# Moving the last weight load into the opening line of loads of a bilinear-interaction kernel, with in-place turning of the third weight part

## The chip, the cores and the metric

One core of one Trainium2 chip. The metric is the device time of one execution in microseconds (us), median over runs. The kernel is already tuned; the question is what one more rearrangement of its opening does.

## The reference, cut to what matters

```python
def _L0_rec_ref(inputs, W):          # inputs (4096, 32, 64), W (496, 64, 64), f32
    F = inputs.shape[1]
    idx_i, idx_j = np.triu_indices(F, k=1)      # 496 pairs i < j
    vi = inputs[:, idx_i, :]
    vj = inputs[:, idx_j, :]
    vidots = jnp.einsum('bpd,pde->bpe', vi, W)
    return vidots * vj                          # (4096, 496, 64) f32
```

The result is 520 MB. It is written once and dwarfs the 34 MB of x and the 8 MB of w.

## The kernel before

The batch is cut into 32 tiles of 128 rows. Per tile, 46 steps each multiply the turned x by up to 16 pairs' weights into PSUM (where TensorE's products land here, `ps<-wT,xT` in the profile), and then multiply by x again into an output buffer `ot`, of which there are three. A group of steps ends with one DMA of about 3 MB to the result. The first three tiles (`LEAD = 3`) run interleaved group by group, because w is still being prepared at that time: it comes in four parts of 128, 128, 128 and 112 pairs, one pair per partition. Each part is ordered (a strided copy into a small buffer `rp`) and turned (TensorE transposes, then a copy out of PSUM into `wT`), in four slices `k` each.

```python
    def load_w(c: int, eng=nc.sync):
        a, b = wrows[c]
        pool, tag = ((opool, "ot"), (opool, "ot"), (const, "w3"), (const, "w3"))[c]
        raw[c] = pool.tile([P, D * D], F32, tag=tag, name=f"raw_{c}")
        eng.dma_start(out=raw[c][: b - a, :], in_=wflat[a:b])
    ...
    load_x(0, nc.sync, 0, 1); load_w(0); load_w(1); load_x(0, nc.sync, 1, NB)   # joined here on one line
    load_w(2)
    new_x(1)
    load_x(1, nc.sync)
    ...
                if (c, k) == (2, NU - 1):
                    load_w(3, nc.scalar)        # the buffer w3 comes free only now
    ...
        if i in aside and c0 == 0 and s not in no_aside:    # shared product
            tmp = tpool.tile([P, CH, 2, E2], F32, tag="tmp", name=f"tmp_{s}")
            nc.scalar.copy(tmp, src)
            nc.gpsimd.tensor_mul(dst, tmp, xj)
        else:
            nc.vector.tensor_mul(dst, src, xj)
```

The third and fourth parts shared one buffer, so the fourth could be loaded only after the third had been ordered. "Shared" products are those that ScalarE and GpSimd make together in place of VectorE.

## Time and profile before

| | before |
|---|---|
| time, median of the first 3 runs | 1342.57 us |
| span in the profile | 1341.7 us |
| busy share: TensorE, VectorE, ScalarE, GpSimd | 85%, 71%, 35%, 40% |
| bytes moved | 562.86 MB, mean 420 GB/s |

How to read it: no compute engine is full (85% at most), DMA is (share 1.00 over the 1229 us from 106 on). In the lines of the profile PE is TensorE (PEld its loads of weights), DVE is VectorE, ACT is ScalarE, POOL is GpSimd, and SPq and ACTq are the queues on which SyncE and ScalarE ask for DMAs. Mean shares hide the opening, where for some microseconds it is not DMA that limits.

### The profile page before, as it was taken

The numbers are of one execution on the slowest core, as the hardware profiler recorded it, in microseconds if no ns is written. First come the engines' busy times: TensorE is split into PE (matmuls) and PEld (weight loads), VectorE is DVE, ScalarE is ACT, GpSimd is POOL, SyncE is SP. The second block draws the span as 40 slices with busy tenths as digits, with TensorE's granted clock in tenths as the row PEclk, the third lists the DMA queues.
The fourth block names the chain that finished last, engine by engine and source line by source line (L and its number), as shares of the span: only waits on it lengthen the run. The fifth ranks groups of instructions, "written<-read, shape, count | busy, mean of one in ns | idle before, by whom it ended". The sixth has DMA issues, their size and how long they took to land.

```text
span 1341.7 us, 16676 instructions
## 1 busy us (share of the span) xinstructions
PE 1137.5 (85%) x6656; PEld 605.0 (45%) x6656; DVE 954.2 (71%) x1262; ACT 467.7 (35%) x623; POOL 543.0 (40%) x252
## 2 busy tenths in 40 slices
PE   5989888878798797998888988788897879988884
PEld 3545444444344444444444544344444435444442
DVE  4778777767677676776767777577775767777774
ACT  4443333333233342333333333333333323333331
POOL 1723343444334443343453434434334433444441
PEclk9989999989999898998999999899998999999997
DMA  9899999999999999999999999999999999999997
GB/s 383 347 428 419 418 425 427 431 422 430 422 432 431 420 430 421 431 424 432 424 415 430 421 432 426 417 430 408 425 429 429 427 421 428 418 416 431 429 432 320
DMA packets 28895, 562.86 MB, mean 420 GB/s; under 512 B 3537, under 2 KB 3537, under 8 KB 3825
## 3 DMA queue, kind: packets, MB, share of 16 engines
q1 hardware_dynamic: 24176, 530.59, 93.0%
q10 hardware_dynamic: 2576, 20.71, 3.8%
q0 software_dynamic: 2064, 10.50, 2.0%
q8 instruction: 52, 0.85, 0.2%
q14 instruction: 27, 0.21, 0.0%
HBM read 41.68 MB, written 520.09 MB: 419 GB/s over the span
## 4 chain that ended last, share of the span: by engine, by line
DMA 55%; PE 22%; DVE 14%; POOL 5%; issue 2%; ACT 1%; SPq 0%; DVEq 0%; POOLq 0%; ACTq 0%
DMA out_dram<-ot 53%; PE ps L248 20%; DVE ot L265 13%; POOL ot L263 4%; DMA xs<-in_r_inputs_dram 2%; PE ptx L146 2%; ACT tmp L262 1%; PE ptw L134 1%; DVE rp L124 0%; POOL rp L124 0%; ACT xT L150 0%; ACT xT L152 0%; ACT xT L151 0%; DVEq L265 0%; POOL xs L100 0%
## 5 line engine op out<-in xcount | busy, mean ns | idle before, releaser
L265 DVE TENSOR_TENSOR ot<-ps,xs 128x1024 f32<-128x1024 f32 (+15 forms) x1252 | 940.9, 807 | 357.1 <-DMA out_dram<-ot 214.9
L248 PE MATMUL ps<-wT,xT 64*128 64x512 f32 (+13 forms) x6016 | 1046.1, 488 | 167.9 <-DVE ot L265 163.3
L263 POOL TENSOR_TENSOR ot<-tmp,xs 128x1024 f32<-128x1024 f32 x220 | 519.4, 2362 | 770.7 <-ACT tmp L262 592.6
L248 PEld LDWEIGHTS ps<-wT,xT 64*128 64x128 f32 x6016 | 534.7, 195 | 620.3 <-DVE ot L265 372.8
L262 ACT COPY tmp<-ps 128x1024 f32<-128x1024 f32 x220 | 222.7, 1012 | 498.0 <-PE ps L248 462.5
L150 ACT COPY xT<-ptx 128x512 f32<-128x512 f32 x128 | 74.9, 585 | 322.8 <-PE ptx L146 322.8
L146 PE MATMUL ptx<-ident,xs 128*128 128x128 f32 x512 | 84.8, 289 | 13.8 <-DMA xs<-in_r_inputs_dram 8.8
L146 PEld LDWEIGHTS ptx<-ident,xs 128*128 128x128 f32 x512 | 54.2, 142 | 85.9 <-DVE ot L265 60.0
L152 ACT COPY xT<-ptx 64x512 f32<-64x512 f32 x128 | 74.5, 582 | 1.5
L151 ACT COPY xT<-ptx 64x512 f32<-64x512 f32 x128 | 73.9, 577 | 1.5
L134 PE MATMUL ptw<-ident,rp 128*128 128x128 f32 (+1 forms) x128 | 19.1, 304 | 4.8 <-DVE rp L124 4.8
L134 PEld LDWEIGHTS ptw<-ident,rp 128*128 128x128 f32 (+1 forms) x128 | 16.1, 160 | 12.5 <-issue 5.4
L138 ACT COPY wT<-ptw 128x1024 f32<-128x1024 f32 (+1 forms) x15 | 14.8, 984 | 20.0 <-PE ptw L134 16.1
L124 DVE COPY rp<-raw 128x1024 f32<-128x1024 f32 (+1 forms) x9 | 12.8, 1453 | 10.6 <-DMA raw<-in_L_rec_W_dram 10.6
L100 POOL DMA_DIRECT2D xs<-in_r_inputs_dram x15 | 9.5, 636 | 0.0
L124 POOL COPY rp<-raw 128x1024 f32<-128x1024 f32 x4 | 8.0, 1990 | 0.1
L124 ACT COPY rp<-raw 112x1024 f32<-112x1024 f32 (+1 forms) x3 | 5.8, 1949 | 4.6 <-POOL ot L263 2.7
L92 POOL DMA_DIRECT2D scratch<-in_r_inputs_dram x7 | 6.2, 888 | 0.3 <-issue 0.3
L138 DVE COPY wT<-ptw 128x1024 f32<-128x1024 f32 x1 | 1.2, 1224 | 2.5 <-PE ptw L134 2.5
L150 ACT ACT_TABLE_LOAD x1 | 1.3, 1283 | 0.7 <-PEq L289 0.7
masks.py:199 POOL TENSOR_SCALAR_AFFINE_SELECT ident<-ident 128x128 f32<-128x128 f32 x1 | 0.3, 292 | 0.1
masks.py:197 POOL MEMSET ident<- 128x128 f32 x1 | 0.2, 204 | 0.3 <-POOLq L289 0.3
(4 smaller groups left out, 0.4 us busy)
## 6 DMA issues: line engine op xcount, KB each, us to landing
out_dram<-ot SPq DMA_DIRECT2D x64, 3360.0 KB, 16.4
out_dram<-ot SPq DMA_DIRECT2D x32, 3168.0 KB, 15.9
out_dram<-ot SPq DMA_DIRECT2D x32, 3104.0 KB, 17.0
out_dram<-ot SPq DMA_DIRECT2D x31, 2880.0 KB, 16.9
xs<-in_r_inputs_dram ACTq DMA_DIRECT2D x9, 2048.0 KB, 25.4
xs<-in_r_inputs_dram POOLq DMA_DIRECT2D x5, 1920.0 KB, 25.0
raw<-in_L_rec_W_dram SPq DMA_DIRECT2D x3, 2048.0 KB, 13.8
xs<-in_r_inputs_dram SPq DMA_DIRECT2D x2, 1024.0 KB, 10.3
```

The costliest lines, as they stand in the source:

```text
L100: tc.keep_in_program_order(nc.gpsimd.dma_start(out=dst[ps, :, fs, :], in_=rows[ps, :, fs, :]))
L124: copy(rp[:r], src[:, k * EU : (k + 1) * EU])
L134: nc.tensor.transpose(pt[:, n, :r], rp[:r, n].rearrange("p h d -> p (h d)"), ident[:r, :r])
L138: copy(wT[home][:, o : o + r, k * EU : (k + 1) * EU], pt[:, :, :r].rearrange("p e r -> p r e"))
L146: nc.tensor.transpose(pt[:, u, :], xs[blk][:, k, f : f + 2, :].rearrange("p f d -> p (f d)"), ident)
L150: copy(xT[:, 0], pt)
L151: copy(xT[D:, 1], pt[:D])
L152: copy(xT[:D, 1], pt[D:])
L248: nc.tensor.matmul(ps[:, h, lo - pa : hi - pa, :], xT[blk, kt, i // RUN][h * D : (h + 1) * D, (i + h) % 2, i % RUN // 2, :], wT[home][h * ...
L262: nc.scalar.copy(tmp, src)
L263: nc.gpsimd.tensor_mul(dst, tmp, xj)
L265: nc.vector.tensor_mul(dst, src, xj)
```

## The change

The intent is to load the fourth part of w at the start, where DMA has a hole. For this the third part's raw rows are loaded straight into the place where its turned form will lie (so buffer w3 is free for the fourth part from the beginning), block 1 of x goes ahead of the third part, the ordering and turning are spread over other steps, and the shared products of the first three tiles use the output buffer itself as their middle stop, since the small buffers are all taken by `rp`.

```diff
     def load_w(c: int):
         a, b = wrows[c]
-        pool, tag = ((opool, "ot"), (opool, "ot"), (const, "w3"), (const, "w3"))[c]
+        if c == 2:
+            raw[c] = home_of(c).rearrange("p r e -> p (r e)")
+        else:
+            pool, tag = (const, "w3") if c == 3 else (opool, "ot")
...
-        copy(rp[:r], src[:, k * EU : (k + 1) * EU])
+        ins = copy(rp[:r], src[:, k * EU : (k + 1) * EU])
+        if c > 0:
+            tc.keep_in_program_order(ins)
...
-        (2, (17, 22, 27, 32), (19, 24, 29, 34)),
-        (3, (54, 54, 55, 55), (57, 60, 63, 66)),
+        (2, (16, 18, 25, 27), (30, 33, 36, 39)),
+        (3, (46, 48, 50, 52), (56, 59, 62, 65)),
...
-    load_w(2)
     new_x(1)
     load_x(1, nc.sync)
+    load_w(2)
+    load_w(3)
...
-                if (c, k) == (2, NU - 1):
-                    load_w(3, nc.scalar)
...
-        if i in aside and c0 == 0 and s not in no_aside:
-            tmp = tpool.tile([P, CH, 2, E2], F32, tag="tmp", name=f"tmp_{s}")
+        if i in aside and c0 == 0:
+            tmp = dst
+            if t >= LEAD:
+                tmp = tpool.tile([P, CH, 2, E2], F32, tag="tmp", name=f"tmp_{s}")
```

(`home_of` returns the part's place in the turned weights; `no_aside`: the list of steps without shared products.)

More of the change, by code (lines that the diff above doesn't have):

```diff
@@ L111, with home_of, load_w @@
     NU = E2 // EU
-    def load_w(c: int, eng=nc.sync):
-        a, b = wrows[c]
-        pool, tag = ((opool, "ot"), (opool, "ot"), (const, "w3"), (const, "w3"))[c]
-        raw[c] = pool.tile([P, D * D], F32, tag=tag, name=f"raw_{c}")
-        eng.dma_start(out=raw[c][: b - a, :], in_=wflat[a:b])
+    def home_of(c: int):
+        home, tag, n = (wrows[3][0], "w3", NP - wrows[3][0]) if c == 3 else (0, "w", wrows[3][0])
+        if home not in wT:
+            wT[home] = const.tile([P, n, E2], F32, tag=tag, name=f"wT_{home}")
+        return wT[home][:, wrows[c][0] - home : wrows[c][1] - home, :]
+    def load_w(c: int):
+        a, b = wrows[c]
+        if c == 2:
+            raw[c] = home_of(c).rearrange("p r e -> p (r e)")
+        else:
+            pool, tag = (const, "w3") if c == 3 else (opool, "ot")
+            raw[c] = pool.tile([P, D * D], F32, tag=tag, name=f"raw_{c}")
+        nc.sync.dma_start(out=raw[c][: b - a, :], in_=wflat[a:b])
     def order_w(c: int, k: int, copy):
@@ L128, in turn_w @@
         r = wrows[c][1] - wrows[c][0]
-        home, tag, n = (wrows[c][0], "w3", r) if c == 3 else (0, "w", wrows[3][0])
-        if home not in wT:
-            wT[home] = const.tile([P, n, E2], F32, tag=tag, name=f"wT_{home}")
         pt = psum.tile([P, EU, P], F32, tag="ps", name=f"ptw_{c}_{k}")
@@ L136, in turn_w @@
             )
-        o = wrows[c][0] - home
-        copy(wT[home][:, o : o + r, k * EU : (k + 1) * EU], pt[:, :, :r].rearrange("p e r -> p r e"))
+        copy(home_of(c)[:, :, k * EU : (k + 1) * EU], pt[:, :, :r].rearrange("p e r -> p r e"))
     def turn_x(blk: int, k: int, q: int, copy):
@@ L192 @@
             due.setdefault(turns[k], []).append(("turn", c, k))
-    no_aside = range(52, 67)
     LATE = 6
@@ L233 @@
                 c, k = args
-                rps[c, k] = order_w(c, k, (v, v, p, v)[c] if k % 2 == 0 else (v, v, p, a)[c])
-                if (c, k) == (2, NU - 1):
-                    load_w(3, nc.scalar)
+                rps[c, k] = order_w(c, k, ((v, v, p, v), (v, v, p, a))[k % 2][c])
         base, end = groups[g]
```

## The prediction

> **What bounds the kernel now.** I read the page's slices first, then the kernel cut into stretches with the DMA share of each, then the order of events around the holes. From the page, the slices of the span (33.5 us each):
>
> ```profile
> PE   5989888878798797998888988788897879988884
> ...
> DMA  9899999999999999999999999999999999999997
> GB/s 383 347 428 419 418 425 427 431 422 430 422 432 431 420 430 421 431 424 432 424 415 430 421 432 426 417 430 408 425 429 429 427 421 428 418 416 431 429 432 320
> ...
> HBM read 41.68 MB, written 520.09 MB: 419 GB/s over the span
> ```
>
> No engine is full, but DMA is, in all slices except the first two and the last. 93% of the bytes are the result, which nothing in the diff makes smaller. So the time is bytes by rate plus the time in which DMA is idle or slow, and the diff touches only the first 100 us. A longer list of stretches shows where the loss is (columns: stretch, length, busy time of PE, PEld, DVE, ACT, POOL with instruction counts, granted clock, DMA share, GB/s):
>
> ```profile
> 28.00:36.00 8.00, 8.00 (x36) 4.14 (x35) 5.15 (x6) 3.77 (x5) 0.74 (x1) 0.79 0.89 368
> 36.00:39.00 3.00, 3.00 (x20) 1.74 (x18) 2.93 (x4) 1.01 (x1) 2.94 (x2) 1.00 0.02 7
> 39.00:60.00 21.00, 21.00 (x121) 11.43 (x118) 15.34 (x16) 10.13 (x10) 17.43 (x9) 1.00 0.99 418
> 60.00:66.00 6.00, 6.00 (x35) 2.97 (x35) 4.14 (x5) 3.77 (x5) 3.65 (x3) 1.00 1.04 316
> 66.00:104.00 38.00, 32.66 (x202) 19.04 (x200) 29.21 (x36) 16.99 (x20) 11.19 (x5) 0.91 1.00 428
> 104.00:106.00 2.00, 2.00 (x16) 0.99 (x14) 2.00 (x4) 1.34 (x3) 1.27 (x1) 1.00 0.62 260
> 106.00:1335.00 1229.00, 1051.53 (x6172) 555.39 (x6168) 882.04 (x1187) 418.84 (x568) 501.73 (x228) 0.95 1.00 425
> 1335.00:1341.70 6.70, 0.00 (x0) 0.00 (x0) 0.00 (x0) 0.00 (x0) 0.00 (x0) 0.50 0.05 21
> ```
>
> The reader is to see three places below 425 GB/s besides the two ends: a hole at 36 to 39 us where nothing is in flight, a slow stretch at 60 to 66 that is nevertheless full, and a small hole at 104 to 106. From 106 on DMA is full at 425. Cut into 2 us pieces, the first hole shows its edges too (26 to 28 us moved 193 GB/s, 34 to 36 moved 204, 38 to 40 moved 184).
>
> What happens there, from the timeline of engines and of the SP queue, and from the chain of waits:
>
> ```profile
> 3.33 24.41 DMA xs<-in_r_inputs_dram
> 27.73 0.14 issue
> 27.87 0.63 PE ptx L146 x4
> ```
> ```profile
> 38.50 0.33 SPq L270 DMA_DIRECT2D out_dram<-ot  x1
> 45.36 0.33 SPq L270 DMA_DIRECT2D out_dram<-ot  x1
> 52.64 0.33 SPq L270 DMA_DIRECT2D out_dram<-ot  x1
> 60.80 0.33 SPq L270 DMA_DIRECT2D out_dram<-ot  x1
> ```
> ```profile
> 58.47 0.40 ACTq L118 DMA_DIRECT2D raw<-in_L_rec_W_dram  x1
> ```
>
> The loads asked for at the start end near 27 us. Two small writes follow (issued at 27.2 and 29.2), and then DMA waits for the compute engines until tile 1's first group is finished at 38.5. TensorE itself waits for block 1 of x until 27.87, since that is last in the line of loads. And w's fourth part, 1792 KB, is loaded only at 58.5, into traffic that is full already.
>
> [...] the load on ACT's queue at 58.5 shares the time with writes and landed about 14.8 us later. [...] VectorE's two copies of w's second part at 21.95 took 4.16 us together while GpSimd multiplied (2.66 us), the one at 34.33 with GpSimd free took 1.05.
>
> **The change part by part.**
>
> 1. The fourth part of w joins the line of loads, and block 1 of x moves ahead of the third part. Nothing is added in bytes; 1792 KB (1.835 MB) move from the busy stretch at 58.5 to the hole. At 425 GB/s they take 4.3 us. The line now ends near 27.0 + 4.3 = 31.3 us, and the first two writes (1952 and 928 KB, 4.7 + 2.2 us), already waiting, follow without the 1 us gap at 27, to 38.2. The next write must be issued about 0.6 us before that, by 37.6. In the kernel before it comes at 38.5.
>
> 2. Block 1 of x lands 4.9 us earlier (it no longer stands behind 2048 KB: 2.097 MB by 425 GB/s), near 22.8 instead of 27.7. TensorE was idle 2.97 us before 27.87 for it. VectorE, the fuller engine at this time, was idle 1.43 and 1.42 us before its multiplies at 30.61 and 33.25, both of which come after that wait; so I take 2.8 us off the 38.5: about 35.7, in time for 37.6. The next (2880 KB, 6.9 us of transfer) is due by 44.5 and should come near 41.5 instead of 45.36. So the hole closes: VectorE and TensorE lead DMA by 2 to 3 us.
>
> 3. What the hole is worth: from 24 to 40 us the eight 2 us pieces moved 438, 193, 500, 375, 393, 204, 11 and 184, mean 287 GB/s, against 425: 16 x 138 / 425 = 5.2 us.
>
> 4. The stretch at 60 to 66: 6 x (425 - 316) / 425 = 1.5 us. It is there only while the fourth part is read among writes, whereas reads in the opening line ran at 411 over 3 to 28 us, edges included. I count 1.5 us as gained, with less certainty.
>
> 5. The hole at 104 to 106: 2 x (425 - 260) / 425 = 0.8 us. It follows the stretch in which ordering (VectorE 2.60 and 1.03 us, ScalarE 1.93 and 1.96) and turning w's fourth part (four times about 1.0 to 1.5 us of TensorE) stood in the steps of tiles 1 and 2, after a wait for the late load. The ordering now comes four to eight steps earlier and its data has long been there. I count it as gained.
>
> 6. Third part turned in place: the same 4 copies on GpSimd (1.99 us), 32 transposes and 4 copies out of PSUM (1.01 us); added is one wait, that all four ordering copies are read before the first turn writes over the raw rows. Those fall at steps 16, 18, 25 and 27, the turn at step 30. GpSimd has 4 x 2.0 + 4 x 2.36 = 17.4 us of work from step 14 to step 27, whereas in the timeline before TensorE takes about 14 us over these steps. By my walk through them the turn waits until 54 us or so, some 2 us late, and tile 1's second group ends near 57.5 for a deadline of about 59. So it is near the path, not on it.
>
> 7. Shared products of the first tiles in the output buffer: 4 multiplies (steps 53, 58, 62, 66) move from VectorE (about 1.1 us each) to ScalarE (1.01) plus GpSimd (2.36). It frees the four small buffers. A ScalarE copy that begins a group must now wait for the output buffer to come free; there the kernel waits for that anyway. Nothing counted.
>
> Sum: 5.2 + 1.5 + 0.8 = 7.5 us at best. A check from the bytes: 562.86 MB at 425 is 1324.4 us, plus 2.5 lost in the first 4 us (45 and 283 GB/s in its halves), plus 6.4 after 1335, gives 1333.3 of span; with the 7.5 it is 1340.8, against a span of 1341.7. So nothing large is missing. I give back 1.4 us for new small gaps (points 6 and 7): 1342.57 - 7.5 + 1.4 = 1336.5 us.
>
> **The rivals.** (a) The gain is only an earlier backlog, and the compute engines, which lose their slack, bring it back later. For it: PE is 85% busy, and later stretches have small dips too (330 GB/s in 1150 to 1154). Against: 1229 us at a share of 1.00. It would leave 1340 to 1342. (b) GpSimd becomes the bound in the opening: the in-place wait holds TensorE by more than my 2 us, in front of three writes of 7.5 us, and the hole reappears around 55 to 65. For it: 17.4 us of work in 14. Against: a lead of 2 to 3 us, and the bytes put ahead. It would give back 2 to 4 us: 1338 to 1341. (c) Only the hole is worth something, the slow stretch is noise of mixed traffic: 1337 to 1338. (d) A different phase of reads against writes moves the rate of 425 by 0.3%, which is 4 us in either direction; nothing in the profile decides that.
>
> **Range and chances.** Rivals a to c pull up, d both ways; best case 1333. So 1333 to 1340.5 eight times in ten. 2% would be 27 us; the whole loss outside the full stretch is under 17 us, so faster by 2% is out of reach, and slower would need a lasting block: 0.01 and 0.01.
>
> **What would show it.** Right: DMA share near 1.00 from 3 to 106 us, no stretch at 7 GB/s; the third output write issued before 37.6 us; no stretch near 316 GB/s after 58 us; 106 us onward still at 425; the write of tile 0's third group issued some 7 us earlier relative to the bytes moved. Wrong: a hole in the list of 2 us pieces after 50 us with TensorE waiting for GpSimd's ordering copies (b), new dips after 106 (a), or a steady rate off 425 by more than 1 GB/s (d).

## The result, and the profile after

The changed kernel took 1338.51 us (median of 4 runs, 1338.19 to 1339.52), the kernel before 1343.04 in the same rounds: ratio 0.9968, 95% interval 0.9953 to 0.9983. Ratios here are the mean time of one kernel's fast runs over the mean of the other's fast runs of the same rounds, so they are not quite the ratio of the medians. The gain is clear of noise and small: 4.5 us by the medians.

The slices of the page of the changed kernel (33.4 us each):

```profile
GB/s 371 431 429 425 426 420 429 423 428 431 424 429 420 421 430 423 431 420 427 432 407 430 424 431 425 422 426 405 429 426 428 426 418 427 422 415 430 430 429 318
```

The second slice went from 347 to 431 GB/s. The first, however, fell from 383 to 371. The stretches that the prediction listed, now for the changed kernel (stretch, length, busy time of PE, PEld, DVE, ACT, POOL, granted clock, DMA share, GB/s):

```profile
28.00:36.00 8.00, 7.02 (x40) 3.54 (x37) 7.63 (x7) 3.53 (x4) 2.36 (x1) 1.00 0.98 325
36.00:39.00 3.00, 2.73 (x15) 1.34 (x16) 3.00 (x4) 0.62 (x1) 0.00 (x0) 1.00 0.95 405
39.00:60.00 21.00, 21.00 (x120) 11.40 (x120) 16.12 (x17) 9.87 (x12) 20.53 (x10) 1.00 1.02 438
60.00:66.00 6.00, 6.00 (x40) 3.60 (x38) 3.80 (x5) 4.23 (x5) 3.93 (x3) 1.00 1.00 430
66.00:104.00 38.00, 34.53 (x236) 19.58 (x234) 30.00 (x37) 23.42 (x28) 23.20 (x10) 1.00 1.01 430
104.00:106.00 2.00, 2.00 (x16) 1.01 (x14) 2.00 (x3) 1.40 (x2) 1.00 (x1) 1.00 1.01 430
106.00:1330.00 1224.00, 1045.47 (x6124) 553.33 (x6120) 877.84 (x1180) 415.32 (x564) 497.25 (x226) 0.95 1.00 424
```

The hole at 36 to 39 (7 GB/s before) is filled, the slow stretch at 60 to 66 (316 before) is gone, and so is the small hole at 104 to 106 (260 before). But a new slow stretch stands at 28 to 36, at a DMA share of 0.98. In pieces of 2 us:

```profile
26.00:28.00 2.00, 2.00 (x13) 1.05 (x12) 2.00 (x3) 1.25 (x3) 0.00 (x0) 1.00 1.10 360
28.00:30.00 2.00, 2.00 (x14) 1.22 (x13) 1.63 (x3) 1.50 (x2) 0.00 (x0) 1.00 1.00 270
...
32.00:34.00 2.00, 2.00 (x16) 1.16 (x12) 2.00 (x2) 0.00 (x0) 2.00 (x1) 1.00 0.94 296
```

(The piece between, 30 to 32, moved 311.) Full engines that move little: 2 x (65 + 155 + 114 + 129) / 425 = 2.2 us are lost there. This is the time in which the fourth part of w is read. The slow stretch was not removed; it moved with the load.

The chain of waits in the opening, changed kernel:

```profile
2.13 15.90 DMA xs<-in_r_inputs_dram
...
26.10 0.59 PE ptx L154 x4
26.69 1.06 PE ps L254 x4
27.75 1.02 PE ptw L143 x8
...
32.94 2.15 DVE rp L134
```

TensorE no longer waits for block 1 of x (the long DMA entry ends at 18.03, the second half of block 0). Where the chain was "DMA until 27.7", it now runs through TensorE and VectorE.

The third write, the first one after the hole, comes at:

```profile
37.21 0.33 SPq L279 DMA_DIRECT2D out_dram<-ot  x1
```

It was 38.50 before. From lists of stretches, the bytes moved by 140 us are 55.3 MB before and 58.0 after; 2.7 MB at 425 GB/s are 6.4 us of lead. At the end of this pair of profiles 4.6 us of it are left (spans 1341.7 and 1337.1).

### The profile page after: what moved, and what is told of

Read it like the earlier page. It is cut to its first block, busy times and chain, and to the rows that moved or that the text cites.

```text
span 1337.1 us, 16689 instructions
## 1 busy us (share of the span) xinstructions
PE 1134.5 (85%) x6656; PEld 604.6 (45%) x6656; DVE 952.7 (71%) x1258; ACT 471.4 (35%) x627; POOL 552.4 (41%) x256
## 4 chain that ended last, share of the span: by engine, by line
DMA 53%; PE 24%; DVE 14%; POOL 4%; issue 2%; ACT 2%; DVEq 0%; SPq 0%; POOLq 0%; ACTq 0%
DMA out_dram<-ot 52%; PE ps L254 22%; DVE ot L274 13%; POOL ot L272 4%; PE ptx L154 2%; DMA xs<-in_r_inputs_dram 1%; PE ptw L143 1%; ACT tmp L271 1%; DVE rp L134 0%; ACT xT L160 0%; ACT xT L158 0%; ACT xT L159 0%; DVEq L274 0%; POOL xs L100 0%; SPq L128 0%
## 5 line engine op out<-in xcount | busy, mean ns | idle before, releaser
L272 POOL TENSOR_TENSOR ot<-tmp,xs 128x1024 f32<-128x1024 f32 x203 | 478.9, 2359 | 705.7 <-ACT tmp L271 532.5
L271 ACT COPY tmp<-ps 128x1024 f32<-128x1024 f32 x203 | 205.5, 1012 | 475.7 <-PE ps L254 432.5
L272 POOL TENSOR_TENSOR ot<-ot,xs 128x1024 f32<-128x1024 f32 x21 | 49.8, 2377 | 51.0 <-ACT ot L271 49.9
L271 ACT COPY ot<-ps 128x1024 f32<-128x1024 f32 x21 | 21.3, 1013 | 24.7 <-PE ps L254 17.1
L134 POOL COPY rp<-wT 128x1024 f32<-128x1024 f32 x4 | 7.8, 1967 | 0.0
```

Of the source, the lines that this page charges most:

```text
L134: ins = copy(rp[:r], src[:, k * EU : (k + 1) * EU])
```

## The experiments

All are edits of the changed kernel unless said otherwise, and all had five timed rounds. "Before" in the table is the kernel before, in the same rounds.

| run | what | us, median | before | ratio | 95% interval |
|---|---|---|---|---|---|
| a_control | changed kernel again | 1339.58 | 1343.14 | 0.9973 | 0.9960 to 0.9985 |
| b_w3_128rows | fourth part as 128 rows | 1338.88 | 1343.14 | 0.9963 | 0.9949 to 0.9977 |
| g_14k | same bytes over 128 partitions | 1338.52 | 1343.14 | 0.9965 | 0.9952 to 0.9977 |
| c_w3_late | late load, went wrong | 1345.96 | 1343.14 | 1.0022 | 1.0009 to 1.0034 |
| c2_w3_late_held | late load, held in order | 1342.53 | 1342.96 | 0.9999 | 0.9986 to 1.0011 |
| d_x1_first | kernel before, x block 1 first | 1341.63 | 1342.96 | 0.9992 | 0.9980 to 1.0005 |
| e_no_aside | no shared products in 3 tiles | 1338.93 | 1342.96 | 0.9973 | 0.9960 to 0.9987 |
| f_hoist1 | second part's ordering not held | 1337.81 | 1342.96 | 0.9964 | 0.9951 to 0.9976 |
| h_128_hoist | b and f together | 1337.52 | 1343.16 | 0.9961 | 0.9948 to 0.9975 |
| a_control2 | changed kernel again | 1338.48 | 1343.16 | 0.9966 | 0.9954 to 0.9979 |

Intervals of the changed kernel and its variants, the two late loads apart, overlap throughout; differences under 1 us between them are not shown by these times. The traces show more.

**The changed kernel again.** No edit.

> The changed kernel again, unaltered. Theory (the saved idle and slow time of DMA is what was gained): median 1338 to 1339 us, 4 to 5 us under the kernel before, and in the profile no hole at 36 to 39 us but a slow stretch near 300 GB/s at 28 to 34 us. If the 1.4 us that the first profile lost again between 400 and 600 us (424 against 427 GB/s) are chance, this profile will not show them there; if they belong to the change, it will.

It came out at 1339.58 us, a little above the expected range. Its profile has the same filled hole and the same slow stretch (360, 270, 319, 297 GB/s from 26 to 34). By 140 us it had moved 57.8 MB, and its span was 1336.2, which is 5.5 us below the kernel before. From 400 to 600 us it ran at 425 GB/s, the first profile of the changed kernel at 424 and the kernel before at 427: 200 x 2 / 425 = 0.9 us lost there, against 1.4. With one profile of the kernel before to set against two, I cannot say whether this belongs to the change or to the run; it stays open.

**The fourth part as 128 rows.**

```diff
         pool, tag = (const, "w3") if c == 3 else (opool, "ot")
+        a = b - P
...   # ordering and transposes over 128 rows, the copy out of PSUM skips the first 16:
-        copy(home_of(c)[:, :, k * EU : (k + 1) * EU], pt[:, :, :r].rearrange("p e r -> p r e"))
+        copy(home_of(c)[:, :, k * EU : (k + 1) * EU], pt[:, :, skip:r].rearrange("p e r -> p r e"))
```

> The fourth part of w loaded as 128 rows (16 rows of the third part again) instead of 112; right result. Theory A (the slow stretch comes from the shape, 112 partitions): the stretch at 26 to 34 us runs near 425 GB/s, the load takes 2.097 MB / 425 = 4.9 us instead of about 6.5, so 1 to 1.6 us less: about 1337. Theory B (it comes from reads that lie next to writes, or from the source): the stretch stays near 300 GB/s and the 0.26 MB more cost 0.6 to 0.9 us: about 1339.2.

The slow stretch went (same columns, kernel with 128 rows):

```profile
26.00:28.00 2.00, 2.00 (x12) 0.91 (x10) 2.00 (x2) 0.67 (x2) 0.23 (x1) 1.00 1.06 451
28.00:30.00 2.00, 2.00 (x14) 1.16 (x12) 2.00 (x3) 1.66 (x4) 0.00 (x0) 1.00 0.96 410
30.00:32.00 2.00, 2.00 (x12) 0.97 (x10) 1.63 (x3) 1.09 (x2) 0.00 (x0) 1.00 1.07 377
32.00:34.00 2.00, 2.00 (x12) 0.84 (x9) 2.00 (x3) 0.61 (x1) 1.31 (x1) 1.00 0.97 407
```

**The same bytes over 128 partitions** (14 KB in each of 128 partitions, in place of 16 KB in 112).

```diff
+        if c == 3:
+            nc.gpsimd.memset(raw[c][:, D * D * 7 // 8 :], 0.0)
+            nc.sync.dma_start(out=raw[c][:, : D * D * 7 // 8], in_=wflat[b - P : b, : D * D * 7 // 8])
+            return
```

> The same number of bytes of w's fourth part as in the changed kernel, but through 128 partitions of 14 KB instead of 112 of 16 KB; wrong result on purpose. Theory A (shape): no slow stretch, 4.3 us for the load, 2 us less: about 1336.5. Theory B (neighbouring writes or the source): nothing changes, 1338.5 and about 300 GB/s at 28 to 34 us.

The result is wrong (relative error 0.65). The four pieces moved 423, 423, 283 and 414 GB/s, so most of the slow stretch went here too, with no byte added. By 66 us this kernel had moved 27.04 MB, the changed one 26.47: 0.57 MB, or 1.3 us at 425 GB/s. The trace's records of single DMA packets say it most directly. One packet is one row of w (the last four lines are from the kernel before and from runs that come further down):

```
rows of w, duration of a packet, ns               median   mean
first to third part, 16 KB, 384 packets (changed)    611    612
fourth part, 16 KB, 112 rows (changed)               923    923
fourth part, 16 KB, 112 rows (a_control)             928    907
fourth part, 16 KB, 112 rows (a_control2)            934    919
fourth part, 16 KB, 128 rows (b_w3_128rows)          614    663
fourth part, 14 KB, 128 rows (g_14k)                 542    634
fourth part, 16 KB, 112 rows, first load (c_w3_late) 912    899
fourth part, 16 KB, 112 rows, late (before)          782    808
fourth part, 16 KB, 112 rows, late (d_x1_first)      785    835
fourth part, 16 KB, 112 rows, late (c2_w3_late_held) 611    722
```

The end of this load is reported 16 times, between 33.78 and 34.49 us. My estimate, with the rows shared evenly among the 16 engines of the profile, seven to each: 7 x 923 = 6.5 us against 7 x 611 = 4.3, and the difference is the 2.2 us lost. From the first packet's start to the last one's end the load took 7.0 us (26.81 to 33.86). For the opening line theory A (shape) holds and theory B (neighbouring writes, or the source) falls: with 128 rows, reads at the same place in the line, next to the same writes, run at nearly full rate (377 to 451 GB/s), and in c_w3_late the 112 rows were as slow (912 ns) with no write near them. But the shape alone does not fix the size of the loss: read late, among writes, the same 112 rows took 782 to 785 ns in two kernels and 611 in a third, where 92 of the 112 stayed under 650. Why they differ is not settled. What in the shape makes a row slow is not shown; that in the opening line the 112-row load takes 1.5 times as long per row is shown (923 ns against 611).

The times, though, fell by 0.7 and 1.1 us only, within noise. In the profile of the 128-row kernel the gain was lost to new holes, at 82 to 84 (177 GB/s) and 92 to 94 (215 GB/s). The second control, further down, shows that these belong to the run and not to the edit.

**A late load, first try.** `load_w(3, nc.scalar)` at step 34.

> One part undone: the fourth part of w is asked for at step 34 on ScalarE's queue as before, everything else as in the changed kernel. Theory (the load fills the hole): loads end at 27 us, the two small writes at about 34, the next write comes at about 37.2, so a hole of about 3.5 us returns and the time is 1341.5 to 1342.5. Rival (the gain comes from block 1 of x landing earlier and from the freed buffers): 1338.5 to 1339.5.

```profile
0.75 0.42 ACTq L128 DMA_DIRECT2D raw<-in_L_rec_W_dram  x1
```

That line, from the timeline of ScalarE, shows that the experiment failed as a test: as the buffer is free from the start, the scheduler put the load in front of everything, at 0.75 us. It then ran beside the first loads of x and w: VectorE's first ordering copy started at 19.58 instead of 10.71, the first write came at 34.07 instead of 25.38, and the kernel was slower than the one before. So on the hole this run speaks neither for the theory nor for the rival. On the shape it says something: the 112 rows were read here from 2.4 to 12.9 us, over 20 us before the first write, and from 4 to 12 us DMA moved 250 to 299 GB/s at a share of 0.91 to 1.08, where the changed kernel moved 426 to 455.

**A late load, held.**

```diff
-    load_w(3)
...
+        if s == 22:
+            load_w(3, nc.scalar)      # with keep_in_program_order on the DMA
```

> The earlier run with a late load failed as a test, since the load was put in front of everything on ScalarE's queue. Here it is held in program order at step 22 (near 45 us); all else as in the changed kernel. Theory (the load fills the hole): first write issued near 25.5 us as in the changed kernel, loads end at 27, the two small writes at 34, the third write is issued near 37.2, so a hole of 3 to 3.5 us near 35 to 38; the slow stretch stands after 46; median 1341.5 to 1342.5. Rival (gain from block 1 of x and from the freed buffers): 1338.5 to 1339.5 in spite of the hole.

1342.53 us, at the upper edge of what the theory expected. The load was issued at 42.88, the first write at 25.49, the third at 37.32, and the hole is back:

```profile
32.00:34.00 2.00, 2.00 (x15) 1.06 (x11) 2.00 (x3) 0.00 (x0) 2.00 (x1) 1.00 0.93 379
34.00:36.00 2.00, 1.12 (x5) 0.29 (x4) 2.00 (x2) 1.01 (x1) 0.28 (x1) 1.00 0.06 22
36.00:38.00 2.00, 1.62 (x8) 0.60 (x8) 2.00 (x3) 0.00 (x0) 0.00 (x0) 1.00 0.00 0
38.00:40.00 2.00, 2.00 (x16) 1.28 (x14) 1.45 (x2) 1.47 (x2) 0.38 (x1) 1.00 1.23 518
```

With everything else of the change in place but this load, the gain is nil (ratio 0.9999), so without the load in the hole the change does not pay. The test is not quite clean, though. By 66 us this kernel had moved 25.00 MB, the changed kernel 26.47 and the kernel before 24.12: the place of the load is worth 1.47 MB or 3.5 us here, and 2.1 us of lead came from the rest of the change. Most of that was lost again in holes (228 GB/s at 86 to 88, 215 and 203 at 94 to 98), after VectorE had waited 4.02 us at 58.91 for an earlier write to free an output buffer. The expected slow stretch was there, but milder: 315, 353, 401 and 396 GB/s from 44 to 52.

**Block 1 of x first, alone** (the kernel before with `load_w(2)` moved behind `load_x(1, nc.sync)`).

> The kernel before with one edit: block 1 of x is loaded ahead of the third part of w. Theory: the third write comes 1.3 to 2.8 us earlier than 38.5, the hole shrinks by as much, 1340.5 to 1342 against 1343. Rival (only the load in the hole counts): 1343.

The third write came at 36.48 instead of 38.50 and the time is 1341.63, 1.3 us lower, in the expected range; the interval includes no change. By 140 us it had moved 56.2 MB, 0.9 more than before. This order shortens the hole but cannot fill it.

**No shared products in the first three tiles.**

```diff
-        if i in aside and c0 == 0:
+        if i in aside and c0 == 0 and t >= LEAD:
```

> The third part of the change taken the other way: in the first three tiles no product goes by ScalarE and GpSimd, all by VectorE (21 multiplies of about 1.1 us more on it, 21 copies and 21 GpSimd multiplies fewer). Theory (VectorE and TensorE have a lead of only 1 to 3 us over DMA in the opening): VectorE, busy 66 of the 84 us from 20 to 104, would need 89, so new holes in DMA, 2 to 5 us slower than the changed kernel: 1341 to 1344. Rival (DMA has ample lead, the place of the shared products is indifferent): 1338.5 to 1339.5.

1338.93 us: not the 1341 to 1344 of the theory. The third write came at 38.27, 1.1 us later, and new holes did appear (82 to 84 at 279 GB/s, 90 to 94 at 329 and 228, 100 to 102 at 210), so that by 140 us it lagged the changed kernel by 0.9 MB, or 2 us. But by 1300 us both had moved 550.7 MB. My theory of the size was wrong, while its holes were there; a lag of 2 us in the opening may vanish by the end, as a lead of 2 us may. By the traces 0.6 MB were made good between 300 and 600 us, where the first profile of the changed kernel ran slightly slower (425 against 427 GB/s), and 0.5 MB between 600 and 900; with one profile of this kernel, that may be chance.

**The second part's ordering not held in program order.**

```diff
-        if c > 0:
+        if c > 1:
             tc.keep_in_program_order(ins)
```

> The changed kernel without the fixed program order of the second part's four ordering copies. Theory: the third write is issued 0.5 to 1.5 us earlier than 37.2 because one copy goes into VectorE's idle time before 19.9; the time is the same within noise (1338 to 1339.5), for DMA is full there anyway. Rival (the third write is on the path): about 1 us faster.

The third write came at 33.91 instead of 37.21, more than expected, and the time is 1337.81 us. The changed kernel itself was not in these rounds; its ratio in its other rounds (0.9966 to 0.9973) lies within this one's interval. DMA had no hole at 34 to 38 in either, which agrees with the theory that the third write is not on the path.

**Both together, and the changed kernel in the same rounds.** The edits are those of b and f.

> Both edits that helped or did no harm together: the fourth part of w as 128 rows, and the second part's ordering copies free to move. Theory: no stretch under 400 GB/s from 4 to 80 us, the third write issued near 34; 0.6 us more bytes, 2.2 us of slow stretch less: 1336.5 to 1338, about 1 us under the changed kernel in the same rounds. Rival (the compute engines have no lead left at 80 to 100 us, so what DMA gains in the opening comes back as holes there): equal to the changed kernel, with holes at 80 to 100.

> The changed kernel once more, in the rounds of the combined one, for a direct comparison: 1338 to 1339.5, and the bytes moved by 140 us within 0.3 MB of 58.0.

1337.52 against 1338.48 us; means of 1337.9 and 1338.7. It is the lowest median of all, and correct, but 0.8 us is inside the intervals. Its four pieces from 26 to 34 moved 401, 418, 360 and 383 GB/s, so the expected "no stretch under 400" did not quite hold.

The second control carried the better lesson. Here are two runs of the same kernel, first a_control, then a_control2 (columns as above; the eighth value is the clock granted to TensorE):

```profile
80.00:82.00 2.00, 2.00 (x19) 1.42 (x17) 1.79 (x3) 0.91 (x1) 0.00 (x0) 1.00 1.00 431
82.00:84.00 2.00, 2.00 (x18) 1.40 (x16) 0.49 (x1) 1.42 (x2) 0.33 (x1) 1.00 1.00 418
92.00:94.00 2.00, 2.00 (x18) 1.24 (x18) 1.45 (x3) 1.59 (x3) 2.00 (x1) 1.00 0.99 418
```
```profile
80.00:82.00 2.00, 2.00 (x10) 1.41 (x8) 1.23 (x1) 0.00 (x0) 0.00 (x0) 0.50 1.03 444
82.00:84.00 2.00, 2.00 (x13) 1.19 (x12) 1.01 (x2) 0.91 (x1) 0.00 (x0) 0.84 0.71 291
92.00:94.00 2.00, 2.00 (x15) 0.87 (x12) 0.98 (x3) 1.06 (x2) 0.89 (x2) 1.00 0.51 215
```

At half clock TensorE makes 10 matmuls in 2 us instead of 19, and DMA runs dry twice, for 2 x (134 + 210) / 425 = 1.6 us. What precedes it is the same in both runs: TensorE waits three times for VectorE, here from a_control2:

```profile
73.08 2.80 PE L254 MATMUL ps<-wT,xT 64*128 64x256 f32 x16 [1.68 <-DVE ot L274]
77.14 0.66 PE L154 MATMUL ptx<-ident,xs 128*128 128x128 f32 x4 [1.26 <-DVE ot L274]
78.27 2.23 PE L254 MATMUL ps<-wT,xT 64*128 64x192 f32 x8 [0.47 <-DVE ot L274]
```

In one run the clock falls after these waits, in the other not. The clock records of the traces show what differs. In each of the twelve traces the clock changes only on a grid of 3.41 us, and the place of this grid differs from run to run (in the first profile of the changed kernel all changes lie within 5 ns of 2.43 us plus whole multiples of 3.413, in that of the kernel before of 1.13 us plus such multiples). In a_control2 one step of it, 75.82 to 79.23, holds 1.26 + 0.47 = 1.73 us of TensorE's idle time, 51%, and the next step runs at half clock; in a_control the same three waits are split over three steps (49%, 37% and 14%), and none follows. Over all twelve traces, from 40 to 1310 us and counted by the records of the matmuls, no step at full clock with under 49% idle time was followed by half clock (3651 steps), every one with over 60% was (273), and between them 55 of 117 were. (In the profiles of the two kernels alone: 0 of 606, 43 of 43, and 12 of 23.) These are counts of these traces; no run changed the idle time alone. The 128-row kernel's profile had the lowered clock too (0.50 at 80 to 82, after a step with 50%), hence its holes at 82 and 92. The two profiled executions took 1338.00 us (a_control) and 1339.46 (a_control2), which is 1.5 apart; the 1.6 us of the two holes, my estimate from their GB/s, are of that size.

## Why the prediction was right or wrong

The predicted time was 1336.5 us with a range of 1333 to 1340.5; measured 1338.51, and over all 14 runs of the changed kernel a mean of 1338.9 against 1343.1 over the 31 of the kernel before. The drop was forecast as 6.1 us and is 4.2 to 4.5. Bound and main mechanism were right, and one term of the sum had the wrong sign.

1. *The fourth part fills the hole.* Right, and shown by its undoing: c2 loses the whole gain in time, 3.5 us of it by 66 us. The moment when DMA runs short was 37.6 by my count; as the load took 6.5 us (the estimate above) instead of 4.3, the loads ended later and the third write, at 37.21, was in time with more to spare than counted. (The 37.6 allows 0.6 us from a write's issue to its first bytes. In the profile before, the first packets of the third write came 0.83 us after its issue at 38.50.)

2. *Block 1 of x lands earlier, third write at 35.7.* Half right. TensorE's wait is gone, but the write came at 37.21: 1.3 us gained, not 2.8. I took VectorE's idle time off as if its work stayed the same. The change fixes the ordering copies in program order, and one of them, which ran at 17.20 in VectorE's idle time before, now runs at 22.10 among its multiplies. Without that fixing (f) the write comes at 33.91. (The fourth write was put at 41.5; by the prediction's own terms it would be 35.7 + 45.36 - 38.50 = 42.6. It came at 43.57, before its deadline of 44.5.)

3. *The hole is worth 5.2 us.* Right within what can be seen: 325 to 438 GB/s in all stretches from 28 to 60, and no empty piece. By 40 us the changed kernel was 1.30 MB or 3.1 us ahead, about the 5.2 less the 2.2 of point 4.

4. *The slow stretch, 1.5 us gained.* This is the step that failed. I held the slowness to be a matter of reading among writes, since other reads in the opening line were fast. It goes with the load's shape, 112 rows: 923 ns per row in the opening line, where 128 rows took 611 to 614, and 912 where no write was near (c_w3_late). So it moved with the load and grew to 2.2 us: 0.7 us lost in place of 1.5 gained. What else sets its size stays open, since in c2 the same rows took 611 ns. The 611 ns packets of the other parts could not have told me, as they all have 128 rows; that the fourth part is the only load of another shape could have.

5. *The hole at 104 to 106, 0.8 us.* Gone in all three profiles of the changed kernel (430 GB/s in the first). But in the second control there are holes at 82 and 92 instead, by the lowered clock, worth 1.6 us. So a gain is left in some runs only.

6. *The in-place wait for all four ordering copies.* The premise was wrong. Slice k of a raw row and slice k of the turned rows lie at the same offsets (element e of each group of 32), so turning slice 0 has to wait for ordering slice 0 alone. ScalarE copies slice 0 out of PSUM while GpSimd has the last ordering copy still ahead (ScalarE, then GpSimd):

```profile
52.19 1.01 ACT L146 COPY wT<-ptw 128x1024 f32<-128x1024 f32 x1
```
```profile
54.51 1.95 POOL L134 COPY rp<-wT 128x1024 f32<-128x1024 f32 x1
```

   With that, rival (b) had no ground: GpSimd is indeed nearly full (20.53 of 21 us from 39 to 60), yet DMA stays at 438 GB/s.

7. *Shared products in the output buffer, nothing counted.* Right in the time: without them (e) it is the same within noise.

The sum with what was measured: 5.2 + 0.8 - 0.7 = 5.3 us, less about 1 that is lost again by the end, gives 4.3. The first profile alone shows more: 6.4 us of lead at 140 us, and 1.8 lost after. The 1.4 us I gave back for new gaps were about right by luck, since the loss came from elsewhere than points 6 and 7: from the lowered clock in some runs, and from small differences over the long rest.

The rivals: (a), the gain comes back as later holes, is partly true. A lead of 6.4 us at 140 us became 4.6, in the first control 5.9 became 5.5, in the second 4.6 became 4.0. (c), only the hole pays, fits the size of the gain, and even a little less came; its reason, that the slow stretch is noise, does not fit, since the stretch came back with the load. (d), the steady rate moved by 0.3%, did not show: 424 against 425 GB/s.

## What to carry to other kernels

When a transfer runs slowly while its engines are full, look at its shape before blaming its neighbours: a load of 112 partitions was slower by its mean than one of 128 wherever it was put here (722 to 923 ns per 16 KB row against 612 to 663, means of the table), though not always by its median (611 in c2_w3_late_held). Here DMA was the bound, and filling a hole of 5.2 us gained 4.2 to 4.5. Such a gain can be checked by putting the load back (c2: ratio 0.9999), held in program order, since with the buffer free the scheduler started the unheld load first, at 0.75 us (c_w3_late). Repeat the profile of the same kernel before explaining a difference of 1 us by an edit.

## What else the traces show

- Here the 112-partition load took 923 ns per 16 KB row in the opening line, 128-partition loads 611 to 614 (medians). By the means, and with the rows shared evenly among 16 engines (my estimate), the whole load of 128 rows took 8 x 663 = 5.3 us and that of 112 rows 7 x 923 = 6.5. Late and among writes the 112-partition load took 611 to 785 (medians).
- Waits of 1.68, 1.26 and 0.47 us within 8 us were followed by a granted clock of 0.50 in one run (a_control2) and 1.00 in another (a_control, where the second took 1.27). In a_control2, 1.73 us of them, 51%, fell into the one 3.41 us step before the lowered clock.
- The tail of the kernel's last DMA is one engine's here, by its rate (my estimate: 430 / 16 = 27): after the last full microsecond (430 GB/s at 1327 to 1328) the changed kernel moves 27 GB/s from 1329 to 1334, in packets of 26880 bytes that take 996 ns each and start one every 993. Of the last write's 16 reports of its end, fifteen come by 1329.92 us and one at 1335.35. In the kernel before the last two come at 1336.71 and 1339.99.

```profile
1330.00:1334.00 4.00, 0.00 (x0) 0.00 (x0) 0.00 (x0) 0.00 (x0) 0.00 (x0) 0.50 0.06 27
```
